# Two short row tiles regrouped as one full tile and 20 rows, the 20 rows multiplied in row and column groups of TensorE

## Chip, cores, metric

One Trainium2 chip, one of its NeuronCores. The metric is the device time of one execution in microseconds (us), smaller is better; the median of several runs is given. Engines: PE is TensorE, DVE VectorE, ACT ScalarE, POOL GpSimd, SP the SyncE queue that issues loads.

## What is computed

Two graph layers on 2708 nodes with 1024 features, all in float32. The reference, cut to what matters:

```python
# layer 0
h = relu(layernorm(x))
f, g = h @ Wf + bf, h @ Wg + bg
scores = where(adj > 0, relu(f @ g.T), NEG)
x = x + softmax(scores, axis=1) @ (h @ W0 + bW)
# layer 1
h = relu(layernorm(x))
hW = h @ W1
e = leaky_relu(hW @ a1 + (hW @ a2).T, 0.2)
x = x + relu(softmax(where(adj > 0, e, NEG), axis=1) @ hW)
```

## The kernel before

**Panels and tiles.** The 2708 rows (as queries) are cut into five panels of 586, 586, 512, 512 and 512. Each panel is cut into row tiles of 128; the two wide panels end with a tile of 74 rows. So there are 22 row tiles, 20 of 128 and two of 74 (`short`).

**Pairs.** As neighbours (the sum over which attention runs) the tiles are taken in pairs: ten pairs of full tiles and, as pair number 2, the two short tiles. A pair is one side of a 2x2 block product that is made with seven products in place of eight (M1, M5, M6, M7, M3, M2, M4), whose sides are sums and differences of the quarter blocks. `NQ` = 11 is the number of pairs, `rows_of[q]` is 128, or 74 for the short pair.

**Stages.** `make_pairs` loads x, normalizes it, transposes it (`h_ps`), makes the seven left sides for the scores (stored in DRAM as `hs_d`) and, with `pair_h`, the seven sides for the aggregation (`hg_d`). Then for every panel p: `project_q` makes B, the seven right sides of the scores, from M = Wf Wg^T; `scores` runs over the pairs, seven products each of four matmuls (contraction 4 x 128), with half the panel's columns (h = 256 or 293) as the moving side, into the banks X (M1, M2), Y (M5, M3) and Z (M6, M7, M4); M4 of a pair is issued behind M1 of the next one (`left_over`). M1 of X is copied out by DVE before M2 is added in the same bank. The result is transposed scores, one tile S per neighbour tile; `finish` adds the mask and keeps the running maximum. `softmax` exponentiates, `aggregate` multiplies with the neighbours' features: seven steps, each a loop over the eleven pairs (k) and four banks (d), with `hc` loaded from `hg_d` as the stationary side; `project` multiplies with W. Layer 1 has no score products (its scores are sums of two vectors f[0] and f[1], made by `weights1`), and the same `aggregate` and `project`. At the end of layer 0 `rows_done` normalizes the finished rows, computes their dots f and (for whole pairs) calls `pair_h` for layer 1.

**Order.** Loads are issued by SP in program order; stores and accumulating loads by POOL. Small pieces of other work (normalizing, masks' maxima, exponentials, dots) wait in a list `later` and are issued behind PE's products by `behind(rate)`. In `scores` the DVE instructions keep the program's order; elsewhere a scheduler places them. [...]`mask_maker` loads adj, makes 0 or -BIG in bf16 (`nm`), and PE transposes it (`mk_ps`). A line of DVE work in the profile is L44, the recording helper; store is L132, the products of scores are L933, those of `project_q` and `aggregate` L489 (names q and g), those of `project` L831.

Of the kernel before, what the change touches and what calls it, by code (L numbers as in the profile page):

```python
# [17 lines left out]
ALPHA = 0.2  # L18
P = 128
W = 512  # L20

# [35 lines left out]
def kernel(  # L57
# [41 lines left out]
    pairs.append(tuple(short))  # L99
# [3 lines left out]
    rows_of = [tiles[a][1] for a, _ in pairs]  # L103
# [39 lines left out]
    groups = [[0, 1], [2], [3, 4], [5, 6], [7, 8], [9, 10]]  # L143
    group_of = {q: (i, j) for i, g in enumerate(groups) for j, q in enumerate(g)}
    assert sorted(group_of) == list(range(NQ)) and all(len(g) == 1 for g in groups if rows_of[g[0]] < P)
    hg_d = [[dram.tile([P, 7, len(g), W], FP, name=f"hg{l}_d{i}") for i, g in enumerate(groups)] for l in range(2)]
    md_d = dram.tile([P, 7, NH, W], FP, name="md_d")
    wt_d = [dram.tile([P, 4, NH, W], FP, name=f"wt{l}_d") for l in range(2)]
    mk_d = [dram.tile([P, NQ, 2, width[p]], BF, name=f"mk_d{p}") for p in range(NP)]
# [9 lines left out]
    nc.vector.memset(ones, 1.0)  # L159
    carry = consts.tile([P, 2, NH, WX - W], FP, name="carry")  # L160
# [102 lines left out]

    def pair_h(l, q, ha, hb):

        n = rows_of[q]
# [18 lines left out]
    made = [0]  # L285

    def make_pairs():
        xs, hT = {}, {}

        def fetch(q):  # L290
            xs[q] = []
            for t in pairs[q]:
                r0, n = tiles[t]
                xs[q].append(row_halves("x", n))
                for e in range(2):
                    load(xs[q][-1][e], x[r0:r0 + n, e * W:(e + 1) * W])
# [5 lines left out]
        def rows(q):  # L302
            pair_h(0, q, *xs[q])

        def transposes(q):
            n = rows_of[q]
            ts = [stream("hsT", (P, 2, NH, P)) for _ in range(4)]
            hT[q] = ts, lambda i: ts[i // 2][:, i % 2, :, :n]
            for k, e, i in ((0, 0, 0), (0, 1, 3), (1, 0, 7), (1, 1, 6)):
                ps = bank("h_ps", (P, NH, P))  # L310
                for c in range(NH):
                    nc.tensor.transpose(ps[:, c, :n], xs[q][k][e][:, c * P:(c + 1) * P], ident[:n, :n])
                nc.scalar.copy(hT[q][1](i), ps[:, :, :n])
                t = pairs[q][k]
                if panel_of[t] == 0:
                    o = tiles[t][0]
                    nc.vector.tensor_copy(first_h[e].rearrange("p (c i) -> p c i", c=NH)[:, :, o:o + n], ps[:, :, :n])

        def sums(q):
            n = rows_of[q]  # L320
# [6 lines left out]
            for g, t in enumerate(ts):  # L327
                o = hs_d[q][:, 2 * g:2 * g + 2]
                if n == P:
                    store(o.rearrange("p m c j -> p (m c j)"), t.rearrange("p m c j -> p (m c j)"))  # L330
                else:
                    store(o[:, :, :, :n].rearrange("p m c j -> p (m c) j"),
                                        t[:, :, :, :n].rearrange("p m c j -> p (m c) j"))

        def dots(q):
            n = rows_of[q]
            for k, t in enumerate(pairs[q]):
# [7 lines left out]
        def last(q):  # L345
            sums(q)
            drop(q, "sums")
            made[0] = q + 1
# [9 lines left out]
        put_norms(0)  # L358
        for q in range(NQ):
            if q + 1 < NQ:  # L360
                put_norms(q + 1)
            put_rows(q)
            put(0.5, lambda q=q: transposes(q), takes_psum=True)
            if q > 1:
                put_dots(q)
            put(2.7, lambda q=q: last(q))
            if q == 1:
                put_dots(0)
                put_dots(1)

    def make_until(q):
        while made[0] <= min(q, NQ - 1):
# [102 lines left out]


    def accumulate(left, right, K, h, order, then, evict, name, prepare={}, rate=0.0, by_k=False):
# [4 lines left out]
        for m in order:  # L482
# [4 lines left out]
            for k, d in ([(k, d) for k in range(K) for d in range(NH)] if by_k else  # L487
                         [(k, d) for d in range(NH) for k in range(K)]):
                nc.tensor.matmul(ps[d], left(m, k, d), right(m, k), start=(start and k == 0), stop=(k == K - 1),  # L489
                                 skip_group_check=True)  # L490
# [784 lines left out]
```

## Time and profile before

| | |
|---|---|
| median of 3 runs | 3178.97 us (3178.84 to 3179.87) |
| the profiled execution, its own time | 3179.79 us |
| its span from first to last instruction | 3178.0 us |
| mean granted TensorE clock | 0.993 |
| score products L933, all | 322.0 + 225.0 + 218.9 us |
| products of an aggregation at 256 columns | seven steps of 19.00 us |
| products of an aggregation at 293 columns | seven steps of 21.71 us |

The profile is of one execution. A row of groups has the line, engine and operation, output<-input names, shapes and count, then busy time in us, the mean of one in ns, and the idle time of the engine ahead of them with what ended it. PE is the matmul, PEld the load of its stationary side. Ends of matmuls are modelled, so lengths of single ones are read with care; starts are measured. A row of waits has total, count, longest.

### The profile page before, as it was taken

What the parts mean: (1) busy time and instruction counts of PE and PEld (TensorE: products, weight loads), DVE (VectorE), ACT (ScalarE), POOL (GpSimd) and SP (SyncE); (2) the same over time, 40 slices, a digit from 0 to 9 for tenths busy, and PEclk for the clock granted to TensorE, in tenths of its full rate; (3) what the DMA queues carried; (4) which work ended last, traced back from release to release, by engine and by line L of the source; (5) the groups of instructions that cost most, each with busy time, mean ns of one, the idle gap of its engine ahead of it and who ended that gap; (6) DMA issues with size and microseconds to landing.
All of it is one profiled execution on the core that took longest, in us unless ns stands there. A gap on an engine that the chain in (4) does not pass through costs nothing.

```text
span 3178.0 us, 35414 instructions
## 1 busy us (share of the span) xinstructions
PE 3114.2 (98%) x12842; PEld 2318.2 (73%) x12842; DVE 1789.0 (56%) x3575; ACT 504.1 (16%) x846; POOL 389.8 (12%) x499
## 2 busy tenths in 40 slices
PE   8999999999999999999999999998999999999998
PEld 5576676667877588886888886865767748778684
DVE  6857676375732686427671368658574472644612
ACT  3412120010200112101020002103031130211200
POOL 3713102110002110011000101020000010000000
PEclk9999999999999999999999999998999999999999
DMA  6958848776546586477755567595655455665655
GB/s 257 325 194 283 293 129 316 218 236 197 169 127 183 174 271 199 149 207 238 238 173 153 160 207 240 190 318 196 197 175 168 149 167 167 189 189 180 203 155 201
DMA packets 286814, 649.92 MB, mean 205 GB/s; under 512 B 53754, under 2 KB 119246, under 8 KB 286640
## 3 DMA queue, kind: packets, MB, share of 16 engines
q1 hardware_dynamic: 246624, 522.95, 52.3%
q0 software_dynamic: 40016, 124.70, 11.4%
q8 instruction: 102, 1.67, 0.2%
q14 instruction: 72, 0.59, 0.1%
HBM read 533.96 MB, written 113.58 MB: 204 GB/s over the span
## 4 chain that ended last, share of the span: by engine, by line
PE 89%; issue 4%; DVE 4%; DMA 1%; POOL 1%; ACT 0%; SPq 0%; POOLq 0%; DVEq 0%; ACTq 0%
PE gy L489 13%; PE gz L489 13%; PE gx L489 12%; PE sz L933 8%; PE pz L831 6%; PE sy L933 5%; PE sx L933 5%; PE gv L489 5%; PE px L831 4%; PE py L831 4%; PE M_ps L424 3%; PE qz L489 3%; PE qy L489 2%; PE qx L489 2%; PE mk_ps L626 1%
## 5 line engine op out<-in xcount | busy, mean ns | idle before, releaser
L933 PE MATMUL sz<-B,As 128*128 128x256 f32 (+3 forms) x1320 | 322.0, 392 | 1.3 <-DVE st L44 1.3
L933 PEld LDWEIGHTS sz<-B,As 128*128 128x128 f32 (+1 forms) x1320 | 244.5, 186 | 58.7 <-DVE st L44 2.2
L933 PE MATMUL sx<-B,As 128*128 128x256 f32 (+3 forms) x880 | 225.0, 399 | 8.0 <-DMA As<-hs_d 8.0
L933 PE MATMUL sy<-B,As 128*128 128x256 f32 (+3 forms) x880 | 218.9, 391 | 0.5 <-DVE st L44 0.5
L765 POOL TENSOR_TENSOR gT<-gT,rr 128x2048 f32<-128x2048 f32 (+3 forms) x20 | 70.1, 3503 | 1168.5 <-DVE rr L44 1085.4
L489 PE MATMUL gx<-P,hc 128*128 128x256 f32 (+3 forms) x880 | 202.7, 392 | 0.3 <-ACT P L1198 0.3
L489 PE MATMUL gy<-T,hc 128*128 128x256 f32 (+3 forms) x880 | 202.5, 391 | 0.0
L489 PE MATMUL gz<-P,hc 128*128 128x256 f32 (+3 forms) x880 | 202.5, 391 | 0.0
L489 PE MATMUL gz<-Sa,hc 128*128 128x256 f32 (+3 forms) x880 | 202.5, 391 | 0.0
L489 PEld LDWEIGHTS gx<-P,hc 128*128 128x128 f32 (+1 forms) x880 | 167.2, 190 | 35.9 <-issue 2.0
L933 PEld LDWEIGHTS sx<-B,As 128*128 128x128 f32 (+1 forms) x880 | 161.2, 188 | 43.8 <-issue 9.9
L489 PEld LDWEIGHTS gz<-Sa,hc 128*128 128x128 f32 (+1 forms) x880 | 167.1, 190 | 33.7
L489 PEld LDWEIGHTS gy<-T,hc 128*128 128x128 f32 (+1 forms) x880 | 166.9, 190 | 34.0
L489 PEld LDWEIGHTS gz<-P,hc 128*128 128x128 f32 (+1 forms) x880 | 166.8, 190 | 33.3
L933 PEld LDWEIGHTS sy<-B,As 128*128 128x128 f32 (+1 forms) x880 | 162.7, 185 | 38.7 <-DVE st L44 1.3
L831 PE MATMUL py<-w,ps 128*128 128x512 f32 (+1 forms) x352 | 155.3, 592 | 0.0
L831 PE MATMUL pz<-w,ps 128*128 128x512 f32 (+1 forms) x352 | 155.1, 592 | 0.0
L627 ACT COPY mask<-mk_ps 128x1024 bf16<-128x1024 bf16 (+1 forms) x55 | 55.7, 1013 | 614.5 <-PE mk_ps L626 324.5
L831 PE MATMUL px<-w,gT 128*128 128x512 f32 x320 | 143.4, 601 | 5.8 <-issue 5.8
L831 PEld LDWEIGHTS pz<-w,ps 128*128 128x128 f32 (+1 forms) x352 | 65.4, 186 | 85.6 <-issue 82.5
L831 PEld LDWEIGHTS py<-w,ps 128*128 128x128 f32 (+1 forms) x352 | 65.4, 186 | 85.1 <-issue 83.2
L831 PEld LDWEIGHTS px<-w,gT 128*128 128x128 f32 x320 | 61.3, 193 | 80.2 <-issue 76.8
(255 smaller groups left out, 4805.3 us busy)
## 6 DMA issues: line engine op xcount, KB each, us to landing
hc<-hg_d SPq DMA_DIRECT2D x350, 512.0 KB
As<-hs_d SPq DMA_DIRECT2D x150, 512.0 KB
w<-wt_d SPq DMA_DIRECT2D x96, 512.0 KB
w<-in_L_gnn_W_dram SPq DMA_DIRECT2D x72, 512.0 KB
md<-md_d SPq DMA_DIRECT2D x56, 512.0 KB
adj_i<-in_adj_dram SPq DMA_DIRECT2D x50, 512.0 KB
hg_d<-g POOLq DMA_DIRECT2D x40, 512.0 KB, 4.8
hs_d<-hsT POOLq DMA_DIRECT2D x40, 512.0 KB, 5.4
```

What stands on the lines that cost most here:

```text
L424: nc.tensor.matmul(ps, wfT[a][c // NH][:, c % NH, :], wgT[b][c], start=(c == 0), stop=(c == NC - 1))
L489: nc.tensor.matmul(ps[d], left(m, k, d), right(m, k), start=(start and k == 0), stop=(k == K - 1), skip_group_check=True)
L626: nc.tensor.transpose(ps[:n, k, i * P:(i + 1) * P], m[0][:, i, k, :n], identb)
L627: nc.scalar.copy(mk[:n, :, :k4 * P], ps[:n, :, :k4 * P])
L765: nc.gpsimd.tensor_tensor(of(e, s), of(e, s), by(s, k), OP.mult)
L831: nc.tensor.matmul(ps, left[i][m][:, k, :], w_[k], start=(start and k == 0), stop=(k == NH - 1), skip_group_check=True)
L933: nc.tensor.matmul(ps[:n, :h], lefts[q][:, i % 2, c, :n], B[m][c // 2][:, c % 2, :h], start=(start and c == 0), stop=(c == NH - 1), skip_g ...
```

## The change

The short pair goes. Its 148 rows become `MONO`, one full tile of 74 + 54 rows, and `TINY`, the last 20 rows. `LEFT` is the number of this unit behind the ten pairs. MONO is multiplied in the plain way (four block products), with sides that exist already: B[M1], B[M2], B[M5], B[M3] in the scores, the halves of h in the aggregation.

In `scores` the transposed 20 rows (`tinyT`, 32 columns with zeros) are the stationary side of four products that lie in the four column groups of the array, each group writing its own 32 partitions of one bank; a product with the 0/1 matrices `pick_lo` and `pick_hi` adds the groups and repeats the 20 rows in every group. So TINY's scores stand in partitions 0, 32, 64 and 96 on. In `aggregate`, `left_over` multiplies MONO with four matmuls and TINY with four more, one for each bank d, each with its own row group, 20 rows deep. For M2, M3 and M4 they are added in the running bank; for M7, whose bank holds a sum that is used twice, they go to banks of their own and are added by DVE (`into_m15`).

`left_h` stores the sides for the aggregation in `hgl_d`; `left_f2` copies the neighbour terms f[1] of the short tiles to columns MONO and TINY by DMAs, and the next DVE instruction makes f2s of them. Masks of TINY are -BIG but for the 20 rows of each group; sums and maxima take TINY once (`once`). The order of making becomes pair 0, pair 1, LEFT, pair 2 and so on.

```diff
--- before.py
+++ after.py
...
-    pairs.append(tuple(short))
...
-    rows_of = [tiles[a][1] for a, _ in pairs]
...
+    n0, n1 = (tiles[t][1] for t in short)
+    NM = P - n0
+    NY = n1 - NM
...
+    LEFT, MONO, TINY = NQ, NT, NT + 1
+    units = pairs + [(MONO, TINY)]
+    order_of_units = [(q, k) for k in range(2) for q in range(NQ)] + [(LEFT, 0), (LEFT, 1)]
...
-    groups = [[0, 1], [2], [3, 4], [5, 6], [7, 8], [9, 10]]
+    groups = [[q, q + 1] for q in range(0, NQ, 2)]
...
+    hsl_d = dram.tile([P, 2, NH, P], FP, name="hsl_d")
+    hgl_d = [dram.tile([P, 2, W + P], FP, name=f"hgl{l}_d") for l in range(2)]
...
+    mk_d = [dram.tile([P, NQ + 1, 2, width[p]], BF, name=f"mk_d{p}") for p in range(NP)]
...
+    tinyT = consts.tile([P, 2, NH, B32], FP, name="tinyT")
+    nc.gpsimd.memset(tinyT, 0.0)
+
+    picks = []
+    for name, gs in (("pick_lo", (0, 1)), ("pick_hi", (0, 2, 3))):
+        t = consts.tile([P, P], FP, name=name)
+        cols = lambda g: ident[:, B32 * g:B32 * (g + 1)]
+        nc.gpsimd.tensor_tensor(t[:, :B32], cols(gs[0]), cols(gs[1]), OP.add)
+        for g in gs[2:]:
+            nc.gpsimd.tensor_tensor(t[:, :B32], t[:, :B32], cols(g), OP.add)
+        for g in range(1, P // B32):
+            nc.gpsimd.tensor_copy(t[:, B32 * g:B32 * (g + 1)], t[:, :B32])
+        picks.append(t)
+    zero = slots.tile([P, WX], FP, tag="slot", name="zero")
+    nc.gpsimd.memset(zero, 0.0)
+    for l in range(2):
+        nc.gpsimd.dma_start(hgl_d[l][:, :, W:], zero[:, :2 * P].rearrange("p (e j) -> p e j", e=2))
...
+    def left_h(l, h0, h1):
+
+        for e in range(2):
+            store(hgl_d[l][:n0, e, :W], h0[e])
+            store(hgl_d[l][n0:, e, :W], h1[e][:NM])
+            for d in range(NH):
+                store(hgl_d[l][B32 * d:B32 * d + NY, e, W:], h1[e][NM:, d * P:(d + 1) * P])
...
-            pair_h(0, q, *xs[q])
+            left_h(0, *xs[q]) if q == LEFT else pair_h(0, q, *xs[q])
...
+            if q == LEFT:
+                two = stream("hsl", (P, 2, NH, P))
+                for e in range(2):
+                    nc.scalar.copy(two[:, e, :, :n0], turned(q, 0, e)[:, :, :n0])
+                    ps = turned(q, 1, e)
+                    nc.scalar.copy(two[:, e, :, n0:], ps[:, :, :NM])
+                    nc.scalar.copy(tinyT[:, e, :, :NY], ps[:, :, NM:n1])
+                store(hsl_d.rearrange("p e c j -> p (e c j)"), two.rearrange("p e c j -> p (e c j)"))
...
+        todo = [0, 1, LEFT] + list(range(2, NQ))
...
-    def accumulate(left, right, K, h, order, then, evict, name, prepare={}, rate=0.0, by_k=False):
+    while not turned_tiles.issuperset(range(len(panels[0]))):
+        one()
+
+
+    def accumulate(left, right, K, h, order, then, evict, name, prepare={}, rate=0.0, by_k=False, more={}):
...
-                nc.tensor.matmul(ps[d], left(m, k, d), right(m, k), start=(start and k == 0), stop=(k == K - 1),
-                                 skip_group_check=True)
+                nc.tensor.matmul(ps[d], left(m, k, d), right(m, k), start=(start and k == 0),
+                                 stop=(k == K - 1 and m not in more), skip_group_check=True)
                 if by_k and d == NH - 1 and k % 3 == 2:
                     behind(rate)
+                if by_k and d == NH - 1 and k == K // 2 and (m, k) in more:
+                    more[m, k]()
...
+                if m in more:
+                    more[m](ps)
...
+            if t in short:
+                for e, side in enumerate((lo, hi)):
+                    load(side[:, :, o:o + NM], hsl_d[:, e, :, n0:])
+                    nc.scalar.copy(side[:, :, o + NM:o + n], tinyT[:, e, :, :NY])
+                continue
...
+                nc.gpsimd.memset(o[:, :, 1], -BIG)
+                negate(o[:n, :, 0], i[:n, :, 0])
+                negate(o[:n, :, 1].rearrange("p i (g c) -> p i g c", c=B32)[:, :, :, :NY],
+                       i[:n, :, 1:2, :NY].to_broadcast([n, r, P // B32, NY]))
...
-            return hc[m, i][:n, j, d * P:(d + 1) * P]
+                load(hc[m, i], hg_d[l][i][:, m])
+            return hc[m, i][:, j, d * P:(d + 1) * P]
+
+        def left_over(ps, e, s, start=False):
+
+
+            two = stream("hl", (P, W + P))
+            load(two, hgl_d[l][:, e])
+            for d in range(NH):
+                nc.tensor.matmul(ps[d], two[:, d * P:(d + 1) * P], S[MONO][:, s], start=start, stop=False,
+                                 skip_group_check=True)
+            for d in range(NH):
+                g = slice(B32 * d, B32 * d + NY)
+                nc.tensor.matmul(ps[d], two[g, W:], S[TINY][g, s], start=False, stop=True, skip_group_check=True)
+
+        def into_m15():
+            ps = [bank(f"gw{d}")[:, :h] for d in range(NH)]
+            left_over(ps, 1, hi, True)
+            for d in range(NH):
+                add(get("m15", d), ps[d], get("m15", d))
 
...
                    {M5: second, M2: fourth, M3: lambda: inverse.append(inverse_sums(p, sm)), M7: scale}, rate=rate,
-                   by_k=True)
+                   by_k=True, more={M2: lambda ps: left_over(ps, 0, lo), M3: lambda ps: left_over(ps, 0, hi),
...
+
+        return NY if units[q][k] == TINY else P
+
...
-            if q + 1 < NQ:
+            if q + 1 <= LEFT:
...
+        sm, st = slot("Sa"), slot("Sb")
+        S[MONO], S[TINY] = sm, st
+        X, Y, Z = (bank(f"s{k}") for k in "xyz")
+        m1, zs = slot("sm1"), slot("sz")
+        t = stream("As", (P, 2, NH, P))
+        load(t.rearrange("p e c j -> p (e c j)"), hsl_d.rearrange("p e c j -> p (e c j)"))
+
+        def part(ps, e, m, start):
+            for c in range(NH):
+                nc.tensor.matmul(ps[:, :h], t[:, e, c], B[m][c // 2][:, c % 2, :h], start=(start and c == 0),
+                                 stop=(c == NH - 1), skip_group_check=True)
+        part(X, 0, M1, True)
+        add(m1[:, hi], X[:, :h], rb[:, hi])
         left_over()
+
+        for c in range(NH):
+            for g, (e, m) in enumerate(((0, M1), (1, M2), (0, M5), (1, M3))):
+                nc.tensor.matmul(Z[B32 * g:B32 * (g + 1), :h], tinyT[:, e, c], B[m][c // 2][:, c % 2, :h], start=(c == 0),
+                                 stop=(c == NH - 1), skip_group_check=True)
+        nc.scalar.copy(zs[:, :h], Z[:, :h])
+        part(X, 1, M2, False)
+        add(sm[:, lo], X[:, :h], rb[:, lo])
+        behind(rate, True)
+        part(Y, 0, M5, True)
+        part(Y, 1, M3, False)
+        add(sm[:, hi], Y[:, :h], m1[:, hi])
+        finish(LEFT, sm, 0)
+        for s, pick in zip((lo, hi), picks):
+            V = bank("sv")
+            nc.tensor.matmul(V[:, :h], pick, zs[:, :h], start=True, stop=True)
+            add(st[:, s], V[:, :h], rb[:, s])
+        finish(LEFT, st, 1)
+        mk_sb.pop((p, LEFT))
+        behind(rate, True)
         nc.hold = False
...
+        order = order_of_units
...
+    def left_f2():
+
+        a, b = (f[1][:, t:t + 1] for t in short)
+        store(f[1][:n0, MONO:MONO + 1], a[:n0])
+        store(f[1][n0:, MONO:MONO + 1], b[:NM])
+        for g in range(P // B32):
+            store(f[1][B32 * g:B32 * g + NY, TINY:TINY + 1], b[NM:n1])
+        nc.vector.tensor_scalar(f2s[:, MONO:], f[1][:, MONO:], ALPHA, None, op0=OP.mult)
...
+        if whole and q == LEFT:
+            put(0.0, lambda: (left_h(1, *(done_rows[s] for s in mine)), left_f2()))
+            put(0.0, met)
...
```

## The prediction

> **What bounds the kernel now.** First the page: who is busy, and which chain ends last.
>
> ```profile
> PE 3114.2 (98%) x12842; PEld 2318.2 (73%) x12842; DVE 1789.0 (56%) x3575; ACT 504.1 (16%) x846; POOL 389.8 (12%) x499
> PE 89%; issue 4%; DVE 4%; DMA 1%; POOL 1%; ACT 0%; SPq 0%; POOLq 0%; DVEq 0%; ACTq 0%
> ```
>
> TensorE is busy 98% of the span and carries 89% of the chain. Then the waits of PE, in total over the span:
>
> ```profile
> PE sx L933 <- DMA As<-hs_d: 8.0, 3, 4.7
> PE mk_ps L626 <- DVE nm L44: 7.5, 6, 2.5
> PE gx L489 <- DMA hc<-hg_d: 6.7, 2, 5.2
> ```
>
> Nothing there recurs: three waits of 8 us together, and so on. So a matmul removed shortens the run by its own time, a matmul added lengthens it, and work on the other engines counts only where it makes PE wait. Then two pieces of the chain in order of time, which price a product, and the groups by form, which price the pieces that the change touches:
>
> ```profile
> 1284.88 19.00 PE gx L489 x88
> ...
> 2391.90 21.71 PE gx L489 x88
> ```
>
> ```profile
> L489 PE MATMUL gx<-P,hc 128*128 128x256 f32 x480 | 105.6, 379 | 0.0
> L489 PE MATMUL gx<-P,hc 74*128 74x256 f32 x48 | 11.4, 379 | 0.0
> L489 PE MATMUL gx<-P,hc 74*128 74x293 f32 x32 | 8.6, 410 | 0.0
> L312 PE MATMUL h_ps<-ident,x 128*128 128x128 f32 x160 | 19.1, 273 | 0.0
> ```
>
> ```profile
> L489 PEld LDWEIGHTS gx<-P,hc 74*128 74x128 f32 x80 | 15.2, 190 | 3.1
> ...
> L933 PEld LDWEIGHTS sx<-B,As 128*74 128x74 f32 x80 | 11.2, 144 | 6.0
> ```
>
> An f32 product is two records of weight load plus matmul: 44 products of one step of the aggregation (11 pairs x 4 banks) are 88 records in 19.00 us, 0.216 us a half and **0.432 us a product at 256 columns**; 21.71/88 gives 0.247 and **0.493 us at 293**. The five panels have 293, 293, 256, 256, 256 columns, so one product done in every panel is 2x0.493 + 3x0.432 = **2.282 us**. Products of the 74-row pair last as long as full ones (379 and 410 ns, the means of full rows): 54 of 128 rows idle.
>
> [...] The trace before has no tiled matmul[...]. It does show how far a matmul reaches beyond its slot: 379 - 216 = 163 ns, and 410 - 247 = 163 ns. [...] No tile here; program order is what every window of PE shows. [...] 190 ns for 74 rows x 128 columns, as for 128x128 in other rows, and 144 ns for 74 columns. [...] The transposes of x (19.1 us/160 = 119 ns each, load after load of 128 columns) show the pace of loads: 119 ns.
>
> **The change part by part.** *Removed and added full products.* In each panel the scores had 7x4 products for the short pair and now have 16 + 2 (the two pick products): 10 fewer. Each aggregation (two layers) had 28 and now has 4x4: 12 fewer. 10 + 2x12 = 34, times 2.282 = **77.6 us removed**. The instruction order of the two built programs agrees: 6898 matmuls of 128x128 become 6728, 50 + 120 fewer.
>
> *Added tiles.* The program order shows 80 matmuls in column groups (16 in a burst, five bursts) and 160 in row groups (4 in a burst, 40 bursts). All packed perfectly they would cost a quarter. But a tile is two halves, high and low, in the same group, issued next to each other, and halves start in order: low 0 must wait for high 0, high 1 stands behind low 0. So only low of one tile and high of the next run together. A tile then costs one half, the last of a burst two. Row tiles load 128 columns twice per step, 2x119 = 238 ns, over the half at 256 (216) and under 293's [...]. Burst of four: 3x0.238 + 0.432 = 1.146 us at 256, 3x0.251 + 0.493 = 1.246 at 293; eight bursts a panel: 24x1.146 + 16x1.246 = 47.4 us. Column burst: 15x0.220 + 0.432 = 3.73, 15x0.251 + 0.493 = 4.26; 3x3.73 + 2x4.26 = 19.7 us. Together **67.1 us added**, so the arithmetic alone is -10.5 us.
>
> *Mode changes.* 45 bursts are entered and left. Not in the trace; bounds: 0 [...] to 163 + 119 ns at each change [...]: 25 us. I take [...] 2x163 + 119 = 0.445 us a burst: **+20.0 us**.
>
> *The wait for f2.* left_f2 copies the neighbour term by DMAs on the POOL queue, ten of them after the second short tile's dot, and the next DVE instruction multiplies the copied columns. It stands in DVE's order ahead of evictions. In the trace before, the place is here:
>
> ```profile
> 1142.94 0.15 DVE L44 TENSOR_SCALAR f2s<-f 74x1 f32<-74x1 f32 x1
> ...
> 1146.21 0.74 DVE L44 SCALAR_TENSOR_TENSOR mx<-mask,f,mx 128x512 f32<-128x512 bf16 x1
> ...
> 1149.40 0.74 DVE L44 TENSOR_TENSOR sm<-sx,rb 128x256 f32<-128x256 f32 x2
> ```
>
> ```profile
> 1135.22 2.15 POOL L132 DMA_DIRECT2D hg_d<-x_res  x4 [0.92 <-ACT x_res L262]
> 1146.17 0.76 POOL L132 DMA_DIRECT2D mk_d<-mask  x1 [8.81 <-ACT mask L627]
> ```
>
> A POOL issue takes 0.54 us (2.15/4). The twenty stores of left_h start near 1135 and end near 1146, hidden. In the new order a mask's store (1146.17) stands ahead of the ten copies: they issue until 1146.9 + 5.4 = 1152.3 and land some 2 to 4 us later (4.1 us is the landing of a 256 KB store), say 1155. DVE waits from 1147 to 1155. Behind it are two maxima (0.8 each) and the copy of X, which PE's M2 needs: about 1157.5. PE has four products, 6.9 us, from 1146.5 until then: 1153.5. **+4 us**, once; bounds 0 and 9.
>
> *Costed at nothing.* Sums of pair_h and sums() for the short pair go; 24 small stores replace 10 + 4 on POOL in the first stage, where 14 more issues (7.6 us) stand against four additions removed (5.6 us) and three hs_d stores (1.6 us). The zero tile and picks run in POOL's idle first 21 us. DVE loses 4 subtractions an aggregation and gains 4 additions for into_m15 at DVE's idlest (11.5 us idle before the evictions of M7). The 22 exponentials stay 22. SP loads 40 hl of 320 KB for 70 hc of 148 KB: equal bytes, as far ahead. The mask's memset on POOL stands right behind the preceding mask's store, a pair ahead of its transposes. Should a cover fail, PE waits a few us in a panel: 0 to 5 us in all.
>
> *Sum.* -77.6 + 67.1 + 20.0 + 4 = **+13.5 us**. The profiled execution took 3179.8 us (span 3178.0, 1.8 around it), 0.8 above the median of 3178.97: 3179.8 + 13.5 - 0.8 = **3192.5 us**.
>
> **The rivals.**
> *Packing for nothing (faster, 0.20).* [...] -10.5 us, or -6.5 with the f2 wait, 3168.5 to 3172.5. [...] Against: the adjacent halves in one group. It decides below (10.5 - 4)/90 = 0.07 us a change.
> *Balance (no difference, 0.20).* Changes at 0.07 to 0.14 us eat the gain: 3173 to 3185.
> *Loads in strict turn (slower, 0.18).* If a group's load waits for the start of the matmul ahead, as every load of the trace does, a row step is a half + 119 ns: 24x1.437 + 16x1.591 = 59.9; column loads of 32 columns cost about 39 ns (144 against 190 ns is 0.83 ns a column): 22.3. Then -77.6 + 82.2 + 20 + 4 = +28.6: 3207.6.
> *No overlap at all (slower, 0.10).* f32 tiles run one after another: 48x2.282 = 109.5, +31.9, with changes and wait +56: 3235. The names of groups alone do not exclude it.
> *The likeliest (0.32)*: 3186 to 3200.
>
> **How the numbers follow.** About 0.2% (6.4 us) is what a measurement of this kernel can tell from no change. Faster 0.20, same 0.20, slower 0.18 + 0.10 + 0.32 = 0.60. The range leaves out full packing and no overlap, some 0.08 and 0.10: 3164 to 3222.
>
> **What would show it.** Right: tile groups whose starts come in pairs [...]; a burst of four near 1.15 us at 256; PE gaps of 0.2 to 0.3 us at both ends of each burst; one DVE wait of 8 us near 1150. Wrong: four starts within 20 ns (full packing), no pairs (strict turn or no overlap, told apart by 335 against 432 ns a tile), no gap at the ends, or a repeated wait of PE in the scores for zs, for hl, or for a POOL memset, which I cost at nothing.

## The result, and the profile after

| | before | after |
|---|---|---|
| median, us | 3179.32 (3178.84 to 3179.87, 4 runs) | 3180.76 (3179.30 to 3186.27, 4 runs) |
| span of the profiled execution, us | 3178.0 | 3178.7 |
| mean granted TensorE clock | 0.993 | 0.991 |

The ratio is 1.0008, with a 95% interval of 0.999 to 1.0025: no difference that can be measured. The prediction had 3192.5 us and a chance of 0.60 for slower. The page of the kernel after, its busy times and its chain:

```profile
PE 3089.0 (97%) x12982; PEld 2283.8 (72%) x12982; DVE 1782.1 (56%) x3561; ACT 504.2 (16%) x855; POOL 406.7 (13%) x547
PE 86%; issue 6%; DVE 3%; DMA 2%; POOL 1%; ACT 0%; SPq 0%; POOLq 0%; DVEq 0%; ACTq 0%
```

PE was busy for 3114.2 us and is now busy for 3089.0: 25.2 us less. The span did not become shorter, so PE stands idle 25.9 us longer (89.7 against 63.8). The change earned something and gave it back as waits. The waits of PE for the whole span (total, count, longest) show where some of them are:

```profile
PE sx L1018 <- DVE sm L45: 11.5, 1, 11.5
PE mk_ps L693 <- DVE nm L45: 8.0, 6, 2.7
...
PE sum_ps L747 <- DVE gT L45: 5.1, 10, 0.5
PE sy L1018 <- DVE st L45: 4.8, 2, 2.6
PE gz L537 <- ACT gT L838: 4.6, 10, 0.5
```

The first is one wait of 11.5 us. `sum_ps` and `gz` are of another kind: ten waits of 0.5 us each, one for every aggregation. None of these three waits was there before. The groups by form price the new instructions (L804 are MONO's products, L808 TINY's row tiles, L1096 its column tiles):

```profile
L804 PE MATMUL gx<-Sa,hl 128*128 128x256 f32 x24 | 5.7, 379 | 0.0
L808 PE MATMUL gx<-Sb,hl 20*128 20x256 f32 x24 | 2.1, 426 | 0.0
L1096 PE MATMUL sz<-B,tinyT 128*32 128x256 f32 x96 | 5.8, 382 | 0.0
```

A lone record of a tile (L808) lasts as long as one of a full product (L804), 426 and 379 ns, yet 24 of the one kind are busy for 2.1 us and 24 of the other for 5.7. Busy time counts what overlaps once, so the tiles overlap. The 96 column records take 5.8 us, a quarter of 96 halves of 0.216 us (20.7) and a little more.

Where the span changed, by stage (from the first product of a stage on PE to the first of the next, after less before):

| stage | us |
|---|---|
| first scores (293 columns) | +2.4 |
| first aggregation | -4.8 |
| second scores (293) | -0.8 |
| third scores (256) | **+13.4** |
| fourth and fifth scores (256) | -2.2 each |
| aggregations at 256 columns, six | -0.8 to -0.9 each |
| other aggregations at 293 columns, three | -1.2 to -1.3 each |
| projection behind the fifth scores | +3.1 |
| all others together | +0.6 |

The gain is spread thin over all stages, and most of the loss is in one place. The following are the PE and DVE timelines there (start, length, instruction, and in brackets the idle time ahead and what ended it):

```profile
1145.43 1.89 PE L1018 MATMUL sy<-B,As 128*128 128x256 f32 x8
1158.78 3.78 PE L1018 MATMUL sx<-B,As 128*128 128x256 f32 x8 [11.46 <-DVE sm L45]
```

```profile
1141.74 0.75 DVE L45 SCALAR_TENSOR_TENSOR mx<-mask,f,mx 128x512 f32<-128x512 bf16 x1
1156.30 0.17 DVE L45 TENSOR_SCALAR f2s<-f 128x2 f32<-128x2 f32 x1 [13.81 <-DMA f<-f]
...
1157.98 0.75 DVE L45 TENSOR_TENSOR sm<-sx,rb 128x256 f32<-128x256 f32 x2
```

DVE waits 13.8 us for the copies of f. The copy of bank X (`sm<-sx`) stands behind them in DVE's order, and PE's M2 needs that copy. The prediction named this chain, with 8 us for DVE and 4 for PE. POOL's timeline says where most of the difference comes from:

```profile
1131.43 4.07 POOL L140 DMA_DIRECT2D hgl_d<-x_res  x8 [1.58 <-ACT x_res L289]
1138.03 4.04 POOL L140 DMA_DIRECT2D hgl_d<-x_res  x8 [2.53 <-DMA hgl_d<-x_res]
1143.24 0.99 POOL L140 DMA_DIRECT2D hgl_d<-x_res  x2 [1.18 <-DMA hgl_d<-x_res]
1144.51 1.01 POOL L140 DMA_DIRECT2D hgl_d<-x_res  x2 [0.27 <-DMA hgl_d<-x_res]
...
1148.84 3.47 POOL L140 DMA_DIRECT2D f<-f  x7 [1.00 <-DMA hgl_d<-x_res]
```

The releaser in the brackets is POOL's own earlier store. Four times POOL waits until one of its stores has landed before it issues the next, 2.53 + 1.18 + 0.27 + 1.00 = 5.0 us in all. What sets off this waiting was not tried. The last issue ends at 1152.3, the last copy takes 4 us to land (the ten took 2.0 to 4.9 us, median 4.1), and f2s starts at 1156.3.

The wait has a second price. The view by stretches (length; busy time of PE, of its loads, of DVE, ACT, POOL; then the granted clock), before the wait and behind it:

```profile
1140.00:1147.00 7.00, 7.00 (x39) 6.12 (x36) 2.42 (x4) 1.01 (x1) 5.55 (x12) 1.00 1.06 392
1158.70:1162.60 3.90, 3.78 (x8) 2.52 (x8) 3.83 (x8) 0.00 (x0) 0.00 (x0) 0.50 0.00 0
```

The same eight halves take 1.89 us ahead of the wait and 3.78 behind it, at half the clock. It is still at half for most of the products at 1164.80, which take 3.09 us in place of 1.89. Together with the transposes between them (1.04 in place of 0.61 us) that is about 3.5 us on top of the 11.5.

### The profile page after: what moved, and what is told of

Same layout as the page of the kernel before. It is cut to its first block, busy times and chain, and to the rows that moved or that the text cites. A ratio compares the mean times of both kernels' runs of the same rounds, so it can differ in the third digit from the quotient of the medians.

```text
span 3178.7 us, 35524 instructions
## 1 busy us (share of the span) xinstructions
PE 3089.0 (97%) x12982; PEld 2283.8 (72%) x12982; DVE 1782.1 (56%) x3561; ACT 504.2 (16%) x855; POOL 406.7 (13%) x547
## 4 chain that ended last, share of the span: by engine, by line
PE 86%; issue 6%; DVE 3%; DMA 2%; POOL 1%; ACT 0%; SPq 0%; POOLq 0%; DVEq 0%; ACTq 0%
PE gy L537 11%; PE gz L537 11%; PE gx L537 11%; PE sz L1018 7%; PE pz L916 6%; PE sy L1018 5%; PE gv L537 5%; PE sx L1018 4%; PE px L916 4%; PE py L916 4%; PE M_ps L469 3%; PE qz L537 3%; PE qx L537 2%; PE qy L537 2%; PE mk_ps L693 1%
## 5 line engine op out<-in xcount | busy, mean ns | idle before, releaser
L1018 PE MATMUL sz<-B,As 128*128 128x256 f32 (+1 forms) x1200 | 296.5, 396 | 4.6 <-DVE st L45 3.4
L1018 PEld LDWEIGHTS sz<-B,As 128*128 128x128 f32 x1200 | 229.2, 192 | 53.3 <-DVE st L45 4.8
L1018 PE MATMUL sx<-B,As 128*128 128x256 f32 (+1 forms) x800 | 203.1, 397 | 16.6 <-DVE sm L45 11.5
L1018 PE MATMUL sy<-B,As 128*128 128x256 f32 (+1 forms) x800 | 201.7, 395 | 4.8 <-DVE st L45 4.8
L537 PE MATMUL gz<-P,hc 128*128 128x256 f32 (+1 forms) x800 | 186.0, 393 | 2.3 <-ACT gT L838 2.3
L537 PE MATMUL gz<-Sa,hc 128*128 128x256 f32 (+1 forms) x800 | 186.0, 393 | 2.3 <-ACT gT L838 2.3
L537 PE MATMUL gx<-P,hc 128*128 128x256 f32 (+1 forms) x800 | 184.4, 392 | 0.3 <-ACT P L1330 0.3
L537 PE MATMUL gy<-T,hc 128*128 128x256 f32 (+1 forms) x800 | 184.2, 391 | 0.0
L1018 PEld LDWEIGHTS sy<-B,As 128*128 128x128 f32 x800 | 152.2, 191 | 37.3 <-DVE st L45 5.9
L537 PEld LDWEIGHTS gx<-P,hc 128*128 128x128 f32 x800 | 152.1, 190 | 32.7 <-issue 2.0
```

The lines of the kernel that those rows point to most:

```text
L1018: nc.tensor.matmul(ps[:n, :h], lefts[q][:, i % 2, c, :n], B[m][c // 2][:, c % 2, :h], start=(start and c == 0), stop=(c == NH - 1), skip_g ...
```

## Experiments

Theory A, formed from the comparison: tiles in different groups run fully at once, entering and leaving a burst costs about 0.2 us each, and what this earns is lost again in three waits: for f2, for the evictions of four banks that end together, and for column maxima that come late. Theories C and D, further down, are about the order in which PE starts tiles. Ratios are to the kernel before, timed again beside each experiment. Times of single stages are from one profiled execution of each kernel.

**1. The copies of f waited for later.** The instruction f2s and the maxima of the left-over tiles move from POOL's copies on to the place of that panel where LEFT's scores begin.

```diff
+    pending = []
+    def left_known():
+        while pending:
+            nc.vector.tensor_scalar(f2s[:, MONO:], f[1][:, MONO:], ALPHA, None, op0=OP.mult)
+            pending.pop()()
...
-        nc.vector.tensor_scalar(f2s[:, MONO:], f[1][:, MONO:], ALPHA, None, op0=OP.mult)
...
-            put(0.0, lambda: (left_h(...), left_f2()))
-            put(0.0, met)
+            put(0.0, lambda: (left_h(...), left_f2(), pending.append(met)))
...
+        left_known()
         sm, st = slot("Sa"), slot("Sb")
```

> The product f2s of the copied columns, and the maxima of LEFT, move from the middle of the third panel's scores to the point where that panel takes LEFT, some 70 us after the copies; nothing else changes. Theory A (DVE, standing in front of the evictions, waits for the landing of the ten copies): the 13.8 us wait of DVE and PE's 11.5 us wait behind it go, the third panel's scores fall from 153.3 us to about 138 (140 before the change, less 2.2), total 3166 us against 3180.8. Rival B (the POOL queue is late as a whole, and its mask stores or loads hold the same scores up): a wait of another name takes its place, the scores stay above 148, total above 3176.

Measured: 3165.93 us, ratio 0.9963 (0.9949 to 0.9976). PE's timeline at the same place:

```profile
1145.96 1.89 PE L1018 MATMUL sy<-B,As 128*128 128x256 f32 x8
1147.69 1.89 PE L1018 MATMUL sx<-B,As 128*128 128x256 f32 x8
```

The product in X follows at once, and no other wait takes the place of the one that went. The third scores fall from 153.31 to 137.45 us, by 15.9: the wait of 11.5 us, some 3.5 us at half the clock, and less than 1 us in the next wait for a mask, which was 1.41 us and is 0.96.

**2. The left-over products in the middle of the step.** For M2, M3 and M4 they are issued after half of the loop over k, as those of M7 are in the changed kernel.

```diff
-                if by_k and d == NH - 1 and k == K // 2 and (m, k) in more:
-                    more[m, k]()
+                if by_k and d == NH - 1 and k == K // 2 and m in more:
+                    more[m](ps)
...
-                if m in more:
-                    more[m](ps)
```

> In M2, M3 and M4 of the aggregation MONO and TINY are added in the middle of the step (behind pair 5 of 10) in place of its end; M7 is as it was. Same products, same bursts. Theory A (four row tiles end together, so the four banks come free together, and the next step's first product and the products of the sums wait for ACT's and DVE's evictions): bursts behind gx and gy fall from 1.37 and 1.41 us to the 0.84 us that the burst of M7 takes at 256 columns, 0.5 us each, 20 bursts: -10.8 us, 3170 us. Rival B (the half microsecond belongs to leaving the tiling mode): each burst keeps 1.35 to 1.4 us, total 3180 to 3182.

Measured: 3169.22 us, ratio 0.9972 (0.9961 to 0.9983). The ten waits for `gz` and the ten for `sum_ps` are gone from the table of waits, and each aggregation is 1.0 us shorter. A burst now costs the same for M2 and M3 as for M7, 0.84 us, so the half microsecond was not the price of leaving the tiled mode. The timeline of PE in the kernel after, and then in the kernel with edits 1 and 2:

```profile
1347.19 0.71 PE L808 MATMUL gx<-Sb,hl 20*128 20x256 f32 x8
1348.39 17.53 PE L537 MATMUL gz<-Sa,hc 128*128 128x256 f32 x80 [0.49 <-ACT gT L838]
```

```profile
1321.86 0.71 PE L806 MATMUL gx<-Sb,hl 20*128 20x256 f32 x8
1322.50 7.17 PE L537 MATMUL gx<-Sb,hc 128*128 128x256 f32 x32
```

The next product starts 1.20 us after the tiles' start in the one and 0.64 us after it in the other. Full products finish the four banks one after another, 0.43 us apart, and each bank is copied out while the next one still runs. Four tiles that run at once finish all four banks together (their last halves start within 20 ns), and the next step has to wait for a copy.

**3. Both edits.**

> Both edits in one kernel. Theory A: the two waits are in different stages and add: 3180.8 - 14.5 - 10.8 = 3155 to 3156 us, 0.7% below the kernel before (3179). Rival B (one hides the other, or loads and DVE come next): less than 15 us of it, above 3165.

Measured: 3154.12 us, ratio 0.9924 (0.9912 to 0.9937). The two gains add up. This kernel is the base of all that follow, the next one excepted.

**4. What a tile costs: the column tiles group by group.** On the kernel after, the two loops of the column burst change places, so that the four tiles of a group stand together.

```diff
-        for c in range(NH):
-            for g, (e, m) in enumerate(((0, M1), (1, M2), (0, M5), (1, M3))):
+        for g, (e, m) in enumerate(((0, M1), (1, M2), (0, M5), (1, M3))):
+            for c in range(NH):
```

> In the scores the sixteen tiles of the 20 rows are issued group by group (four in column group 0, then four in group 1 and so on) in place of round and round. Theory A (tiles meet only if they stand next to each other in the program, the queue does not look past a tile of a busy group): nearly one after another, 16 x 0.432 = 6.9 us at 256 columns against 2.06, 7.9 against 2.31 at 293: 3 x 4.85 + 2 x 5.6 = +25.7 us, 3206 us. Rival B (PE takes from its queue what fits a free group): 2.1 to 2.6 us a burst, total within 3 us of 3181.

Measured: 3197.27 us, ratio 1.0058 (1.0043 to 1.0074), between the two expectations, so that neither holds. Here and below, the cost of a burst is counted on PE's records: from the start of the last half ahead of it to the start of the second half behind it, less two halves. In rounds (the kernel after) it is 2.06 us at 256 columns and 2.31 at 293; group by group it is 4.73 and 5.35. With 0.41 us for the mode changes and 0.216 us a half, 4.73 is 20 halves in a row: more than the 8 of full overlap and less than the 29 of strict program order (where only a group's last half and the next one's first run together). So some halves start ahead of one that stands before them in the program, but not all that could. Two accounts, both estimates of mine from the times of the row burst (0.84 us) and of these two orders (2.06 and 4.73), fit: a window of four instructions in program order (theory C), or a place for four halves in each group, one running and three waiting, filled in program order (theory D).

**5. Two tiles of a group at a time.**

```diff
-        for c in range(NH):
-            for g, (e, m) in enumerate(((0, M1), (1, M2), (0, M5), (1, M3))):
+        for c2 in range(2):
+            for g, c, e, m in [(g, 2 * c2 + i, e, m) for g, (e, m) in enumerate(((0, M1), (1, M2), (0, M5), (1, M3)))
+                               for i in range(2)]:
```

> On the kernel with both edits, the column burst is issued two tiles of a group at a time (0 0 1 1 2 2 3 3, twice). Theory C (PE looks at the next four waiting matmul halves and starts the first whose group is free; this window gives 2 slots of a half for a row burst, 8 for the burst in rounds and 20 for the burst by groups, as measured): 11 slots, 11 x 0.216 + 0.34 to 0.41 = 2.71 to 2.79 us at 256 columns, about 3.06 to 3.12 at 293, where rounds take 2.06 and 2.31: +3.7 us, 3158 us. A window of three would give 14 slots (3.4 us), of five 10 (2.5 us), no look-ahead 25 slots (5.8 us, +19 us).

Measured: 3156.41 us, ratio 0.9931 (0.9916 to 0.9945). The burst is 2.10 us at 256 columns and 2.35 at 293, hardly more than in rounds. Theory C needs 11 halves, 2.7 us or more, and falls. Theory D has four halves of each group in its place and needs 8, 1.73 us and the mode changes. (The whole run is 2.3 us longer than that of experiment 3, within the intervals; 1.7 us of it are in the second scores, which experiment 11 comes to.) But theory D was made to fit these orders, so a new one had to test it.

**6. Three tiles of a group, then the fourth of each.** In the expectations, `e3_both` is the kernel of experiment 3. The queue of four halves is theory D's estimate, from the 2.06, 2.10 and 4.73 us above.

```diff
+        for some in (range(NH - 1), range(NH - 1, NH)):
+            for g, c, e, m in [(g, c, e, m) for g, (e, m) in enumerate(((0, M1), (1, M2), (0, M5), (1, M3)))
+                               for c in some]:
```

> On the kernel of e3_both, the column burst is issued three tiles of a group at a time (c = 0, 1, 2 of group 0, then of group 1, 2, 3; then c = 3 of each group). Theory D (TensorE issues in program order into a queue of four halves per group, one running and three waiting): a group's six halves hold up the next group by two slots, so the groups start 0, 2, 4, 6 slots late, group 3 ends its eight halves at slot 14: burst = 14 x 0.216 + 0.39 = 3.41 us at 256 columns and 14 x 0.247 + 0.39 = 3.85 at 293, against 2.06 and 2.31 in rounds; the run is 3 x 1.35 + 2 x 1.54 = 7.1 us longer than e3_both, 3161. A queue of five or of three per group gives 11 or 17 slots: 2.77 or 4.06 us at 256. Rival, only whole groups in a row matter and not the number waiting: 8 slots, 2.1 us, 3154.

Measured: 3160.94 us, ratio 0.9943 (0.9926 to 0.9959). The burst is 3.43 us at 256 columns and 3.86 at 293, against 3.41 and 3.85 of theory D. PE's timeline of that burst, in this kernel, then in rounds (edits 1 and 2 alone), then group by group:

```profile
1221.32 3.30 PE L1096 MATMUL sz<-B,tinyT 128*32 128x256 f32 x32
```

```profile
1217.91 1.93 PE L1095 MATMUL sz<-B,tinyT 128*32 128x256 f32 x32
```

```profile
1244.86 4.60 PE L1096 MATMUL sz<-B,tinyT 128*32 128x256 f32 x32
```

The same 32 records take 3.30, 1.93 and 4.60 us, by order alone. The records do not name the group, but in the first order the first four loads of 106 ns (those between them have 108 to 110) start at 1221.314, 1221.775, 1222.237 and 1222.699. If these are the first loads of the four groups, each group begins 0.46 us, about two halves, after the one before, as theory D has it.

**7. All four row tiles in one group.** The computation is changed as the expectation says.

```diff
-                g = slice(B32 * d, B32 * d + NY)
+                g = slice(0, NY)
```

> On the kernel with both edits, the four row tiles of a burst all lie in row group 0 (they read the 20 rows of group 0, so the columns of the first feature block are added to all four banks: a part of the computation is changed). Same instructions, same tiling mode. Theory A (the saving is that the four groups run at once; the mode change costs 0.41 us a burst whatever runs inside): a burst takes 8 x 0.216 + 0.41 = 2.14 us at 256 columns, 8 x 0.247 + 0.41 = 2.38 at 293, against 0.84 and 0.90: 24 x 1.30 + 16 x 1.48 = +55 us, 3209 us. Rival (the tiles are short because they are 20 rows deep, not because they run at once): 3154 to 3158 us.

Measured: 3208.69 us, ratio 1.0094 (1.0079 to 1.0109). Tiles that are 20 rows deep are thus not short for that reason, as the expectation's rival had it.

**8. The row tiles as full products.** The computation is changed here too.

```diff
-                g = slice(B32 * d, B32 * d + NY)
+                g = slice(0, P)
```

> On the kernel with both edits, the four row tiles of a burst become products over all 128 rows of the same operands, with no row groups (the four feature blocks are added up in every bank: a part of the computation is changed). No mode change is left in the aggregation. Theory A: a burst takes 8 halves, 1.73 us at 256 columns and 1.97 at 293: 24 x 0.886 + 16 x 1.07 = +38 us against the kernel with both edits, 3192 us; and 40 x 0.41 = 16.4 us less than with all tiles in group 0, which is the price of the mode changes. Rival (mode changes are nearly free, the 0.41 us is the load of the first tile): the two differ by less than 5 us.

Measured: 3190.02 us, ratio 1.0038 (1.0025 to 1.0051). PE's timelines of the same burst, of experiment 7 and then of 8:

```profile
1332.22 1.99 PE L806 MATMUL gx<-Sb,hl 20*128 20x256 f32 x8
1334.14 7.17 PE L537 MATMUL gx<-Sb,hc 128*128 128x256 f32 x32
```

```profile
1327.79 1.89 PE L806 MATMUL gx<-Sb,hl 128*128 128x256 f32 x8
1329.52 7.07 PE L537 MATMUL gx<-Sb,hc 128*128 128x256 f32 x32
```

By records, the burst is 2.12 us in one group, 1.73 as full products, and 0.84 in four groups. The first two differ by 0.39 us, although both are eight halves in a row: that is the price of going into the tiled mode and back. In four groups, 0.84 is two halves (0.43) and that price (0.41). So the four tiles overlap without any loss, and half of what they cost is the change of mode. By this, tiles in one group would cost more than no tiles.

**9. The picks ahead, and less made ahead.** In the kernel with both edits, the projection behind the fifth scores still took 54.24 us where it had taken 49.45, and the first scores 189.9 us where they had taken 184.7. The pick products and the finishing of TINY move behind M5, and `make_until` runs one pair less ahead (LEFT comes between, so that q + 2 meant one more thing to make).

```diff
-            make_until(q + 2)
+            make_until(q + 1)
...
         part(Y, 0, M5, True)
+        for s, pick in zip((lo, hi), picks):
+            V = bank("sv")
+            nc.tensor.matmul(V[:, :h], pick, zs[:, :h], start=True, stop=True)
+            add(st[:, s], V[:, :h], rb[:, s])
+        finish(LEFT, st, 1)
         part(Y, 1, M3, False)
```

> On the kernel with both edits: the two pick products and the finish of the 20 rows are issued behind M5 of MONO, in place of the end of the panel's scores, and the scores ask for pairs made up to q+1 in place of q+2. Theory A (the fourth project step waits 2.5 us for the column maxima, because DVE takes the 20 rows last; the first scores lose 5 us, because one pair more is to be made by DVE ahead of each step): 54.2 us of that project step fall to 50 or 51, 189.9 us of the first scores to 184 to 186, total 3146 to 3150 us. Rival (both are loads and DVE work that only move): within 2 us of 3154.

Measured: 3148.00 us, ratio 0.9905 (0.989 to 0.992), the fastest of all kernels here. The projection is back at 49.45. The first scores took 187.0, where 184 to 186 had been expected. The waits for DVE fell there, but those for loads (`As`) rose from 6.7 to 12.7 us. Two more runs took the halves of this edit apart.

**10. Only the picks ahead.** `e8_early_picks` in the expectations is experiment 9, and the projection that "follows the fourth scores" is the one behind the fifth.

> On the kernel of e3_both, only the second part of e8_early_picks' neighbour: the pick products and TINY's maximum stand behind M5, make_until(q + 2) stays. Theory A (the column maxima come late because TINY's finish is last): the projection that follows the fourth scores falls from 54.24 to 49.45, the first scores stay at 189.9 and the second at 158.5: 3154.1 - 4.8 = 3149.3. Rival (the late maxima were cured by making less ahead): 54.2 stays, 3154.

Measured: 3150.06 us, ratio 0.9912 (0.9898 to 0.9927). The projection takes 49.45 us and the first scores 189.8: the whole of the 4.8 us is the picks' place. The waits of PE around that projection, in the kernel with edits 1 and 2 alone, are the following; with the picks ahead, this row is gone:

```profile
PE sp_ps L251 <- DVE mcol L45: 2.7, 2, 2.3
```

TINY's scores were the last to be finished in the panel, the column maxima `mcol` need them, and the spreading of the maxima stood in PE's way. These 2.7 us of waits stand in all ten kernels that have the picks at the end. In seven of them a stretch at half the clock follows, in most of 3.4 us, and the projection takes 54.2 us or more; in three (the changed kernel and experiments 1 and 7) none follows, and it takes 52.5. The second scores took 1.7 us longer, which the expectation did not have; the next run shows the same and is read there.

**11. Only less made ahead.**

> On the kernel of e3_both, only the other part of e8_early_picks: make_until(q + 1) in place of q + 2, as far ahead in pairs as the kernel before was. Theory A (DVE has one pair more to make ahead, LEFT, in the first scores): first scores 189.9 to about 187.0, waits of PE for DVE st 8.2 to about 2.4, second scores +1.75, the projection stays at 54.2: 3154.1 - 1.2 = 3153. Rival (the picks moved ahead are what eased the first scores in e8): first scores stay at 189.9, 3154.1.

Measured: 3151.43 us, ratio 0.9916 (0.9901 to 0.993). The first scores took 185.4 us, and the projection stayed at 54.24. PE's waits in this stage, first with edits 1 and 2 alone, then with less made ahead:

```profile
PE sx L1016 <- DMA As<-hs_d: 6.7, 2, 4.1
PE sy L1016 <- DVE st L45: 4.8, 2, 2.6
PE sz L1016 <- DVE st L45: 3.4, 2, 3.0
```

```profile
PE sx L1016 <- DMA As<-hs_d: 13.9, 4, 7.2
PE sy L1016 <- DVE st L45: 1.9, 1, 1.9
...
PE sz L1016 <- DVE st L45: 0.4, 1, 0.4
```

The waits for DVE fall from 8.2 to 2.3 us, as theory A said, but the waits for loads grow by 7.2. The view by stretches, with the same columns as above, shows what else differs:

```profile
204.59:394.50 189.91, 172.69 (x810) 130.89 (x809) 129.56 (x249) 33.13 (x60) 49.57 (x65) 0.96 0.78 268
```

```profile
205.43:390.87 185.44, 168.59 (x811) 128.68 (x810) 126.13 (x249) 33.24 (x60) 49.60 (x65) 0.97 0.80 274
```

PE's idle time is 17.2 us in the one and 16.9 in the other. What differs is its busy time, 4.1 us less for as many products, and the granted clock. PE's records count it: 30 halves of the score products run at half the clock in the first, in four stretches, and 11 in the second, in one stretch. 19 halves at 0.25 us more each are 4.7 us; the stage is 4.5 shorter. So the shorter time of this execution is not the reason that the theory gave: PE waited as long, and the clock fell less often.

Whether the edit brings that about isn't shown. The kernel after and that of experiment 8 have the same program in this stage as the one with edits 1 and 2, and took 187.0 and 187.1 us, no more than experiment 9 with less made ahead (187.0); in the kernel after, 17 halves ran at half the clock. What the edit does show is that it moves the waits: 5.7 to 8.2 us for DVE in the ten kernels that make more ahead, 2.4 and 2.3 in the two that make less. The medians with less made ahead are 2.1 and 2.7 us lower (experiment 9 against 10, 11 against 3), within the intervals.

The second scores' 1.7 us in the last two runs are of the same kind: the wait of 2.7 to 2.8 us for a mask stands in all these kernels, but behind it 6 halves run at half the clock in this run, 7 in the kernel after, and none in the kernel with edits 1 and 2. Where the clock falls there, it is for one stretch of 3.4 us, and half of that is lost. Which of such short waits lowers the clock was not settled.

## Why the prediction was wrong, step by step

**What bounds the kernel: right.** Products removed shortened the stages by their own time. In the fourth and fifth scores, 10 products of 0.432 less a burst of 2.06 are -2.26 us; -2.19 and -2.21 were measured. In an aggregation at 256 columns, 12 products less four bursts of 0.841 are -1.82; with the evictions covered it was -1.84. The 77.6 us removed stand.

**Added tiles: the step that failed.** The prediction had 67.1 us, because the low half of a tile waits for its high half, and the high half of the next tile "stands behind low 0". The first part is right and the second is not. Here is the start of a burst in the kernel after, as PE's records have it (start in us, load or matmul, its name):

```
2674.403                    MM, the last full half
2674.711  LD  gx<-P,hl      2674.712  MM
2674.717  LD                2674.719  MM
2674.724  LD                2674.726  MM
2674.731  LD                2674.732  MM
2674.819, .826, .832, .839  LD, the second halves
2675.032, .039, .046, .052  MM, the second halves
```

The first halves of all four groups start within 20 ns, 7 ns apart, and only then come the four second halves. (In one group halves follow 0.216 us apart, experiment 7, so these four lie in four groups.) The loads overlap too, four of 181 ns within 20 ns, where the prediction had each tile pay for its two loads in turn. The prediction's own list had this as a sign that it was wrong ("four starts within 20 ns (full packing)"). Measured, two halves a row burst and eight a column burst are 24 x 0.432 + 16 x 0.493 + 3 x 1.73 + 2 x 1.97 = 27.4 us, 40 us less than predicted. The trace before shows full products in program order, a half every 0.216 us at 256 columns; that tiles in different groups keep that order was my estimate, which no trace had shown. Experiments 4 to 6 show that it does not hold for these f32 tiles: group by group, strict order would take 29 halves and the mode changes, 6.7 us, and 4.73 were measured. Theory D's account, four halves of each group placed ahead of need, fits all four orders (2.06, 2.10, 3.43 and 4.73 us); it is an estimate from these times, and no record shows the places. The prediction's steps of 0.251 and 0.220 us add some ns to a half (0.247 and 0.216), which no trace had shown either; the starts came 7 ns apart.

**Mode changes: right in total, not in its parts.** The prediction took 0.445 us a burst, +20.0. Measured were 0.41 us in the 40 row bursts and 0.34 in the five column bursts: 18.1 us. That PE waits at a change is seen in the burst above: the first tile load starts 0.308 us after the last full matmul's start, where an ordinary load starts 0.002 us after it. But the prediction had 0.282 us on entry (163 + 119 ns) and 0.163 on leaving, an estimate from a matmul's reach beyond its slot and the pace of loads; that a change costs anything was not shown by the trace before. In the row bursts of the kernel with both edits each is about 0.2 us at 256 columns, in two steps: the first half behind the change starts 0.30 to 0.31 us after the last one ahead of it, and the second half 0.32 us after the first, where 0.216 is usual.

**The wait for f2: right in kind, too small.** +4 us, bounds 0 and 9; it was 15.6 (the third scores lost 13.4 where 2.2 were to be won). The stage begins 4.55 us earlier in the kernel after than in the one before (1091.04 against 1095.59), so this is added to compare with the prediction's times. DVE began to wait at 1142.5 + 4.55 = 1147.0, exactly as predicted. The last copy was issued at 1156.9 and not at 1152.3, 4.6 us later, because POOL waited for its own stores, which the prediction didn't have. It landed 4.0 us later and not 2.7: 1.3 us. PE's products ran out at 1151.9 and not at 1153.5: 1.6 us. With the 4 us predicted, that is the 11.5 us of PE's wait. The rest is the clock behind the wait, at which I had not looked: the granted clock was 0.50 for over 7 us behind it, with one short wait of 1.41 us in that time. Half-clock stretches also stand behind some waits of 2.3 to 2.8 us (experiments 10 and 11).

**Costed at nothing: partly right.** `into_m15` was hidden (the burst of M7 costs 0.841 us, with no wait behind it), and so were nearly all loads of hl (one wait of 1.6 us). Three things were not on the list. Evictions behind M2 and M3 cost 10 us, at 1.0 an aggregation: I looked at DVE's additions for M7, and not at the fact that banks which used to end in turn now end together. TINY's place at the end of the scores cost 3.1 us, and 4.8 in kernels where the clock fell behind the wait. First and second scores lost 5.0 and 1.9 us against the sum of their products. In the second it is the clock (7 halves at half speed). In the first, PE's idle time grew by 4.3 us, waits for DVE in place of some for loads, and that was not undone by any run. Two figures of the prediction are wrong without consequence: 40 loads of 320 KB are 12.8 MB and 70 of 148 KB are 10.4, not equal bytes, yet PE waited less for hc and hl together (4.7 us) than for hc before (6.7); and 46 ns over 54 columns, in the rival of the loads, are 0.85 ns a column, not 0.83.

**The sum.** -77.6 + 27.4 + 18.1 = -32.1 us by arithmetic, then +15.6 (f2), +10 (evictions), +3.1 (late maxima), +5.0 and +1.9 (first and second scores), -3.6 (the first aggregation waited less for hc than before, beyond the arithmetic), +0.6 elsewhere: +0.5. The two spans differ by +0.7. Against the +13.5 predicted, the tiles and mode changes came out 41.6 us lower and everything else 28.6 us higher.

**The rivals.** "Balance" named the right time, 3173 to 3185, for a wrong reason: it needs mode changes of 0.07 to 0.14 us. "Packing for nothing" kept the 67.1 us of the tiles and took the mode changes as free; 27.4 and 18.1 us were measured, so it was wrong in both parts, and in its 3168.5 to 3172.5. Full packing, to which the prediction gave some 0.08, is what the tiles showed. That packing could be full and the gain go to waits elsewhere was no rival of mine, though each part was within sight: the wait for f2 was my own step, and the evictions were in every step of the trace before. "No overlap" and "loads in strict turn" fell with the first timeline. The range of 3164 to 3222 held the time by luck, because errors of some 42 and 29 us had opposite signs.

## What to carry to other kernels

Products that don't fill the array are worth packing into groups, but a burst paid 0.34 to 0.41 us here for the mode changes: it wins only where the halves that it saves take longer than that. Tiles of one group should not stand more than two deep (four halves) before another group's: one, two, three and four deep, the column burst took 2.06, 2.10, 3.43 and 4.73 us at 256 columns. Price what the packed products do to their neighbours as carefully as the products: they end together, so their evictions come together (1.0 us an aggregation here), and they should stand in the middle of a step with other products behind them. An instruction that waits for a small DMA copy belongs as far behind the copy's issue as its first reader allows; here one misplaced wait, with the half clock behind it, took back 15.6 us, half of the 32 that the packing had won.

## What the runs showed of the hardware

- f32 tiles: each was two halves of load and matmul. Halves in different groups overlapped without loss: 2 x 0.216 us for four row tiles, in a burst of 0.84 us with the mode changes, the first four starts within 20 ns. Within a group they followed one another at 0.216 us at 256 columns (a burst of 2.12 us).
- Order of tiles: four orders of the same 16 column tiles took 2.06, 2.10, 3.43 and 4.73 us at 256 columns. An estimate from the first, second and fourth of these has about four halves of each group placed in program order and a fifth hold up all behind it; it had 3.41 us for the third. It gives 8, 8, 14 and 20 halves and 0.34 to 0.41 us for the mode changes.
- Going into a tiled mode and out of it cost about 0.2 us each, whether the tiles overlapped (0.41 a burst) or not (0.39).
- A wait of 11.5 us cost PE about 3.5 us more afterwards, at half the clock (0.50 granted). Waits of 2.3 to 2.8 us were followed by a stretch of 3.4 us at half the clock, a loss of 1.7 us, in some runs and not in others, at the same place of the program too (one such wait in seven kernels of ten).
- On the POOL queue, copies of about 0.2 KB or less within SBUF took 2.0 to 4.9 us to land, 4.1 in the median, and POOL's issues waited up to 2.5 us for its own earlier stores.
